# A projection's short piece in one PSUM bank, and a quarter of the values product moved ahead of the next scores

## The chip, the cores and the metric

The kernel runs on one NeuronCore of a Trainium2 chip. Its engines work side by side, each through its own queue in order: TensorE multiplies matrices (PE in the profile, with PEld for its weight loads), VectorE (DVE) and ScalarE (ACT) read results out of TensorE's accumulation memory (PSUM) and work on them, GpSimd (POOL) works on on-chip tiles only, and SyncE (SP) issues the DMA transfers. The metric is the device time of one execution in microseconds; lower is better. Before the change it is 3225.41 us, the median of three runs (3222.88 to 3227.68).

## The reference

The input is 8 images of 512 channels and 32 x 32 = 1024 positions, all in float32. Two blocks follow one another:

```python
# layer 0: multi-head attention, 8 heads of 64 channels
hn  = group_norm(x, gn1)                       # 32 groups
qkv = einsum('bchw,oc->bohw', hn, w_qkv) + b_qkv
q, k, v = split(qkv per head)
wgt = softmax(einsum('bct,bcs->bts', q*s, k*s))   # 1024 x 1024 per head, s = 64 ** -0.25
a   = einsum('bts,bcs->bct', wgt, v)
x   = x + group_norm(einsum(a, w_proj) + b_proj, gn2)
# layer 1: one attention over all 512 channels, weights normalised by row
qkv = einsum('oc,bcn->bon', w_qkv, x);  qkv = qkv / (rms over channels + 1e-4)
attn = softmax(q^T k / sqrt(512));  h = w_out @ (attn applied to v)
out = (x + h) / sqrt(2)
```

What the change touches are the projections q and k of layer 0 and the product `a`.

## The kernel before, in words

The images are taken one after the other (batch 0 to 7). For each the heads of layer 0 go in four **pairs** (j = 0 to 3, two heads side by side on the 128 rows of the array), and each pair in eight **steps** of 128 query positions, so a batch has 32 steps (i = 8 j + r). The loop over steps starts at line 1234; it collects small functions in the lists `fill`, `early` and `later`, and `Heads.step` (line 630) runs one step:

1. `softmax(i)`: for each of the two heads VectorE takes the row maxima of the scores (nm<-s) and ScalarE the exponentials (p<-s).
2. `values` of a group of two steps, on every second step from step 5 on (LAG is 5): TensorE multiplies the turned probabilities pT of the group by v, 8 blocks of positions by 2 heads, into one bank; ScalarE then writes the result to `a`.
3. the functions of `fill`: at most one piece of the next pair's projections.
4. `scores(i + 1)`: TensorE, four products of half the array's rows each.
5. `turn`: VectorE transposes the probabilities of the step before (pb<-p) and SP issues four transfers that finish the turning (pT<-pb).
6. `early`, `scale` (GpSimd divides by the row sums, p<-p), and `later`, in which GpSimd does the additions that a piece has asked for.

TensorE's order is therefore values, piece, next scores. All engines run in the order of the program, except that each waits for what it needs.

PSUM is split in two pools. Scores and other wide results take three tiles of two banks each (`ps_s`): two hold one step's scores, so the second head's scores of the next step need a tile that the first head's exponential has freed. Everything else goes through two single banks taken in turn (`ps_m`, the function `bank`, line 114).

From batch 1 on q and k of pairs 1 to 3 come from `project_seven` (line 474): by a scheme of seven products in place of eight, in four pieces n = 0 to 3. A piece is made of half-array matmuls, upper 64 rows into one bank and lower 64 rows into the other, which run two at a time. Pieces 1 to 3 have four products a half, piece 0 (the **short piece**) has two. ScalarE copies both banks of the short piece out, and GpSimd adds the copies to get one temporary, `tmp[1]`. The short piece of pair j + 1 is made at the first step of pair j: steps 0, 8 and 16. Pair 0 of the following batch uses `project_rows` in steps 24 to 31, as batch 0 does throughout.

At step 0 to 2 of a batch the last three products of layer 1 of the batch before (`Layer1.products(1, c)`, po<-e) stand in front of the piece in the same list, each in a single bank; VectorE reads each of them out in `later` (`keep`).

The weights of pair 3's and of the next batch's pair 0's projections are fetched at steps 8 and 16 (`fetch_qk`, line 257), in SP's queue in front of that step's transfers of probabilities.

Of the kernel before, what the change touches and what calls it, by code (L numbers as in the profile page):

```python
# [52 lines left out]
def attention_blocks_kernel(  # L53
# [29 lines left out]
    CI, NT, HN = C // P, N // P, N // 2  # L83
# [21 lines left out]
    PE, VE, AC, PO, SY = (InOrder(tc, e) for e in (nc.tensor, nc.vector, nc.scalar, nc.gpsimd, nc.sync))  # L105
# [8 lines left out]
    def bank(name, n=HN):  # L114
        return ps_m.tile([P, n], F32, tag="mm", name=name)

    def matmuls(pm, terms):

        for k, (lhsT, rhs) in enumerate(terms):
            PE.matmul(pm, lhsT, rhs, start=(k == 0), stop=(k == len(terms) - 1))  # L120
            if k % 2:
                yield

    def run(pieces):
        for _ in pieces:
            pass
# [32 lines left out]
    rows = const.tile([GQKV, P], F32, name="rows")  # L159
# [208 lines left out]
    RG, TG = 2, 2 * P  # L368
    NB = N // P
    STEPS, LAG = CI * NB, 5  # L370
    halves = (slice(0, D), slice(D, P))
# [62 lines left out]
    class Sums:  # L434
# [31 lines left out]

        def right(self, half, n, k):

            rows = halves[half]
            if n == 0 or (n, half) in ((1, 0), (3, 1)):  # L470
                return self.hn[rows, k, HN:] if n == 0 else self.hn[rows, k, :HN]
            return (self.t24 if n + half == 2 else self.t3)[rows, k]

    def project_seven(b, j, right):

        qk = pair.tile([P, 2, N], F32, tag="qk", name=f"qk_{b}_{j}")
        kp = qk[:, 1, :].rearrange("p (be m) -> p be m", be=4)
        w, tmp = near["qk7"][:, (j - 1) % 2], [near["v#"][:, k * HN : (k + 1) * HN] for k in range(3)]  # L480

        def turned(t):
            return t.rearrange("p (m be) -> p be m", be=4)

        q1, q2 = (qk[:, 0, th * HN : (th + 1) * HN] for th in range(2))
        k1, k2 = (kp[:, :, th * P : (th + 1) * P] for th in range(2))

        def add(to, a, b_):
            return lambda: PO.tensor_add(to, a, b_)

        adds = (
            ([add(tmp[1], tmp[1], tmp[0])], []),
            ([], []),
            ([add(q2, q2, q1), add(k2, k2, turned(q2))], [add(k1, k1, k2), add(k2, k2, turned(tmp[1]))]),
            ([add(q1, q1, tmp[0]), add(q2, q2, tmp[1])], [add(q2, q2, tmp[2])]),
        )

        def pieces():
            for n in range(4):
                pms = [bank(f"pq7_{b}_{j}_{n}_{r}") for r in range(2)]  # L500
                count, at = (CI, CI * n - 2) if n else (2, 0)
                for k in range(count):
                    for r in range(2):
                        PE.matmul(pms[r], w[halves[r], at + k, :], right(r, n, k), start=(k == 0), stop=(k == count - 1))
                if n == 0:
                    AC.copy(tmp[1], pms[0])
                    AC.copy(tmp[0], pms[1])
                elif n == 1:
                    AC.activation(q1, pms[0], AF.Identity, bias=bqs[:, j : j + 1])
                    AC.copy(k1, turned(pms[1]))  # L510
                elif n == 2:

                    AC.copy(q2, pms[0])
                    AC.activation(k2, turned(pms[1]), AF.Identity, bias=bkq[:, j : j + 1])
                else:
                    AC.copy(tmp[0], pms[1])
                    AC.copy(tmp[2], pms[0])
                yield adds[n]

        return qk, pieces()  # L520
# [30 lines left out]
    class Heads:  # L551
        def __init__(self, b, hn, v, qk):
            self.b, self.hn, self.v, self.a = b, hn, v, None
            self.qk = {0: qk}
            self.pT, self.ps, self.waiting = {}, None, None

        def scores(self, i):
            j, r = divmod(i, NB)
# [47 lines left out]
                PO.tensor_scalar(p[:, :, hh, :], p[:, :, hh, :], tot[:, hh : hh + 1], 1.0, ALU.mult, ALU.mult)  # L606
            self.waiting = (i, p)

        def values(self, g):

            j, t0 = g // (NB // RG), g % (NB // RG) * TG
            po = bank(f"po0_{self.b}_{g}", TG)
            if self.a is None:
                self.a = big(f"a_{self.b}")
            for s in range(NT):
                for hh in range(2):
                    ch = (2 * j + hh) * D
                    PE.matmul(
                        po[halves[hh], :],
                        self.v[:, s, ch : ch + D],  # L620
                        self.pT[g][:, :, :, hh, s, :],
                        start=(s == 0),
                        stop=(s == NT - 1),
                    )

            AC.activation(self.a[:, j, t0 : t0 + TG], po, AF.Identity, bias=col(BV, j))
            slots.give(f"pT_{self.b}_{g}")
            del self.pT[g]
# [110 lines left out]
    class Seven:  # L739
# [8 lines left out]
        half, drains, held = None, [], False  # L748
# [478 lines left out]
    heads, norm1, hn_next = Heads(0, x0, v0_0, qk0), None, None  # L1227
# [3 lines left out]
    for b in range(B):  # L1231
        hn, more = heads.hn, b + 1 < B
        todo, due, rest = iter(()), [], []
        for i in range(STEPS):
            j, r = divmod(i, NB)
            due = rest

            projects = (i - LAG) % RG if not b or i not in (2, 3) else i == 3

            def project():  # L1240
                nonlocal due, rest
                now, rest = next(todo, None) or ([], [])
                due = due + now

            rest, fill = [], [project] if projects else []
            early, later = [], []
            if i < CI:
                fill, later = fills[i] + fill, laters[i]
            if r == 0:
                if j + 1 < CI:  # L1250
                    heads.qk[j + 1], todo = project_seven(b, j + 1, one.next.right) if b else project_rows(
                        b, j + 1, hn, near["v#"]
                    )
                elif more:
                    qk_next, todo = project_rows(b + 1, 0, hn_next, place("spare", b))
                if j + 1 == CI:
                    slots.give(f"hn_{b}")
                    if not more:
                        o_last = big(f"o_{b}")
                        todo = project_out_half(b, heads, o_last)  # L1260
            later.append(lambda: [f() for f in due])

            if b and more and i in (1, 2, 9, 10):
                later.append(lambda: norm1.apply((1, 2, 9, 10).index(i), PO))
            if not b:


                if i == CI:
                    hn_next = big(f"hn_{b + 1}")
                    norm1 = Norm1(b + 1, hn_next)  # L1270
                if 0 <= i - CI < CI:
                    later.append(lambda: load_x(b + 1, hn_next, i - CI))
                if 0 <= i - CI - 2 < 2 * CI:
                    later.append(lambda: norm1.stats((i - CI - 2) // 2, i % 2))
                k = i - 3 * CI - 2
                if k == 0:
                    coeffs = norm1.gn.all_steps()
                    early += [norm1.aggregate, lambda: next(coeffs)]
                elif 0 < k < 8:
                    early.append(lambda: next(coeffs, None))  # L1280
                if 0 <= k - 7 < CI // 2:
                    for ci in range(2):
                        later.append(lambda ci=ci: norm1.apply(2 * (k - 7) + ci, PO))

            if b and i == NB:
                fetch_qk(CI - 1, b)
            if b and i == 2 * NB and more:
                fetch_qk(CI, b)
            if b and i == STEPS - NB - 3 and not more:
                fetch("proj", b)  # L1290
            m, odd = divmod(i - STEPS + NB, 2)
            if more and m >= 0:

                if m < 2:
                    k = slice(2 * (i - STEPS + NB), min(2 * (i - STEPS + NB) + 2, 7))
                    SY.dma_start(out=near["v7"][:, k], in_=far["v7"][:, k])
                if i == STEPS - NB:
                    tv = big(f"tv_{b + 1}").rearrange("p (k i) (h n) -> p k i h n", k=2, h=2)
                    right_v = RightSide(hn_next, tv[:, 0], tv[:, 1])
                    sums_v = (None for ci in range(CI) for _ in right_v.sum_steps(ci, PO))  # L1300
                later.append(lambda: next(sums_v, None))

            if not more and i == STEPS - 4:
                xt = big(f"x_{b}")
            if not more and m in (2, 3) and not odd:
                load_x(b, xt, m - 2)
            heads.step(i, fill, early, later)
# [123 lines left out]
```

## Time and profile before

| | |
|---|---|
| median of three runs | 3225.41 us |
| the profiled execution | 3224.11 us, of which its span is 3222.0 us |
| granted TensorE clock | 0.998 |
| PE busy | 3192.6 us, 99% of the span |
| DVE, POOL, ACT busy | 2279.2, 1253.2, 1045.5 us |
| matmul records pq (all projections by seven products) | 1176, mean 589 to 592 ns |
| ACT copies v<-pq | 84, 592 ns each |
| POOL additions v<-v, 128 x 512 | 21, 1275 ns each |

The profile is of one execution. A row of the timeline gives the start and the time in us, the engine, the line, the operation, what it writes and reads, and in brackets the idle time before it and what ended that; equal neighbours are merged (x8). Every instruction is recorded by one helper at line 34 of the program (`InOrder`), so every row says L34 and the tiles tell rows apart: s scores, nm row maxima, p probabilities, pb and pT their turned forms, pq the pieces of `project_seven`, po both kinds of values product (po<-pT in layer 0, po<-e in layer 1). One float32 matmul of the program is two records. A matmul's recorded end is modelled, so the distance between starts is the better measure.

### The profile page before, as it was taken

Reading aid. Unit: us, or ns where it says so; the run is one execution under the profiler, and the core shown is the slowest. Engines: PE = TensorE matmul, PEld = TensorE weight load, DVE = VectorE, ACT = ScalarE, POOL = GpSimd, SP = SyncE. Lnnn points to the kernel's source line nnn. Section 1 sums busy time; section 2 is a strip of 40 time slices with the busy share of each in tenths; the row PEclk is TensorE's granted clock in tenths of the full one; section 3 lists DMA queues with packets and bytes.
Section 4 is the critical chain, followed back from the end, with each engine's and each line's share of the span. In section 5 each row is a group of like instructions: output and inputs, shape, how many; then the busy total and the mean of one; then the engine's idle time right before and its main releaser. Section 6 shows DMA issues by size and latency. Waiting matters only on the chain.

```text
span 3222.0 us, 36603 instructions
## 1 busy us (share of the span) xinstructions
PE 3192.6 (99%) x13218; PEld 1645.9 (51%) x13218; DVE 2279.2 (71%) x3166; ACT 1045.5 (32%) x1813; POOL 1253.2 (39%) x1025
## 2 busy tenths in 40 slices
PE   8999999999999999999999999999999999999899
PEld 5455644455444554545544555445554556444354
DVE  5697767876678765886658866587766877578652
ACT  2453114521145211551215512254023531145210
POOL 1554224732257212671227613265223642246121
PEclk9999999999999999999999999999999999999999
DMA  6777225862168512784228832388224872158600
GB/s 203 206 204 219 76 56 155 215 200 59 56 182 226 179 43 62 203 229 142 53 85 213 224 111 52 107 215 235 92 58 112 216 220 75 30 156 211 187 7 33
DMA packets 225180, 451.57 MB, mean 140 GB/s; under 512 B 21572, under 2 KB 62056, under 8 KB 219112
## 3 DMA queue, kind: packets, MB, share of 16 engines
q1 hardware_dynamic: 224880, 449.20, 49.7%
q8 instruction: 106, 1.74, 0.2%
q14 instruction: 74, 0.61, 0.1%
q10 hardware_dynamic: 120, 0.02, 0.0%
HBM read 137.26 MB, written 29.56 MB: 52 GB/s over the span
## 4 chain that ended last, share of the span: by engine, by line
PE 93%; DMA 3%; DVE 2%; SPq 1%; issue 1%; POOL 1%; DVEq 0%; ACTq 0%; POOLq 0%
PE po L34 26%; PE s L34 13%; PE pq L34 7%; PE p_e_T L34 7%; PE p_v_T L34 6%; PE p_e_B L34 5%; PE p_v_B L34 5%; PE pqk L34 4%; PE py L34 4%; PE p_u_T L34 3%; PE p_o_T L34 3%; PE p_u_B L34 3%; PE p_o_B L34 2%; DMA pT<-pb 2%; DVE pb L34 1%; PE pv L34 1%
## 5 line engine op out<-in xcount | busy, mean ns | idle before, releaser
L34 POOL TENSOR_SCALAR p<-p,tt 128x1024 f32<-128x1024 f32 x512 | 566.0, 1118 | 742.0 <-DVE tt L34 729.6
L34 ACT ACTIVATE p<-s,nm 128x1024 f32<-128x1024 f32 x512 | 565.6, 1109 | 876.3 <-DVE nm L34 534.0
L34 DVE TENSOR_REDUCE nm<-s 128x1 f32<-128x1024 f32 x512 | 602.2, 1217 | 151.7 <-PE s L34 151.0
L34 DVE STREAM_TRANSPOSE pb<-p 128x2048 f32<-128x2048 f32 x256 | 589.9, 2304 | 50.3 <-DMA pT<-pb 27.8
L34 PE MATMUL s<-qk 64*128 64x512 f32 x2048 | 524.0, 604 | 1.1 <-POOL qk L34 0.5
L34 PE MATMUL po<-pT,v 128*64 128x256 f32 x4096 | 471.8, 383 | 3.1 <-DMA pT<-pb 3.0
L34 PE MATMUL po<-e,v 128*128 128x512 f32 x1024 | 450.8, 596 | 0.0
L34 PEld LDWEIGHTS po<-pT,v 128*64 128x64 f32 x4096 | 285.1, 137 | 221.0 <-ACT v L34 31.8
L34 PEld LDWEIGHTS s<-qk 64*128 64x128 f32 x2048 | 200.5, 186 | 250.7 <-issue 222.2
L34 PEld LDWEIGHTS po<-e,v 128*128 128x128 f32 x1024 | 191.4, 190 | 241.1 <-issue 241.1
L34 PE MATMUL pq<-hn,qk 64*128 64x512 f32 x504 | 197.1, 592 | 0.0
L34 POOL TENSOR_TENSOR esum<-esum,e 128x512 f32<-128x512 f32 x96 | 130.5, 1360 | 154.3 <-ACT e L34 151.8
L34 POOL TENSOR_TENSOR u<-u,xy 128x512 f32<-128x512 f32 x64 | 79.2, 1268 | 280.9 <-DMA xy<-far_rinv 275.4
L34 POOL TENSOR_TENSOR x<-x,o 128x1024 f32<-128x1024 f32 x21 | 52.1, 2512 | 348.5 <-ACT o L34 348.5
L34 ACT ACTIVATE e<-e,shift,rinv 128x512 f32<-128x512 f32 x128 | 100.9, 812 | 256.7 <-DVE e L34 256.7
L34 DVE TENSOR_TENSOR e<-e,p_e_T 128x512 f32<-128x512 f32 x160 | 107.0, 685 | 86.5 <-PE p_e_T L34 84.3
L34 DVE TENSOR_TENSOR v<-v,p_v_T 128x256 f32<-128x256 f32 x300 | 114.3, 417 | 68.7 <-PE p_v_T L34 50.0
L34 PE MATMUL pqk<-hn,qk 64*128 64x512 f32 (+1 forms) x672 | 158.2, 590 | 0.0
L34 PE MATMUL pq<-v,qk 64*128 64x512 f32 x336 | 150.9, 589 | 0.0
L34 PE MATMUL pq<-t,qk 64*128 64x512 f32 x336 | 150.9, 589 | 0.0
L34 PE MATMUL p_e_T<-s,t 128*128 128x512 f32 x320 | 147.8, 592 | 0.0
L34 PE MATMUL py<-x,gram 128*128 128x512 f32 x320 | 140.3, 598 | 5.4 <-issue 5.4
(222 smaller groups left out, 4096.7 us busy)
## 6 DMA issues: line engine op xcount, KB each, us to landing
pT<-pb SPq DMA_DIRECT2D x1024, 256.0 KB, 4.6
qk<-far_qk SPq DMA_DIRECT2D x21, 896.0 KB
hn<-in_x_dram SPq DMA_DIRECT2D x32, 512.0 KB, 4.6
x<-in_x_dram SPq DMA_DIRECT2D x32, 512.0 KB, 3.6
out_dram<-x SPq DMA_DIRECT2D x32, 512.0 KB, 4.6
score<-far_score SPq DMA_DIRECT2D x8, 1792.0 KB
value<-far_value SPq DMA_DIRECT2D x8, 1792.0 KB
proj<-far_proj SPq DMA_DIRECT2D x7, 1792.0 KB
```

The source lines that it names most:

```text
L34: return lambda *args, **kw: self._pin(call(*args, **kw))
```

## The change

The short piece is made with the whole array: two matmuls over all 128 rows into one bank, copied to `tmp[1]` by one ScalarE instruction; the second bank, the second copy and the addition go. `Heads.values` can now be called for part of its blocks: with `most=2` it does the first two of eight blocks and keeps the bank open for the next call. In batches 1 to 7, at the first step of pairs 1 and 2 (steps 8 and 16), such a call is put behind the short piece, that is ahead of the next scores; the rest of that group follows at the next step, where the whole of it stood.

```diff
         def right(self, half, n, k):
 
+            if n == 0:
+                return self.hn[:, k, HN:]
             rows = halves[half]
-            if n == 0 or (n, half) in ((1, 0), (3, 1)):
-                return self.hn[rows, k, HN:] if n == 0 else self.hn[rows, k, :HN]
+            if (n, half) in ((1, 0), (3, 1)):
+                return self.hn[rows, k, :HN]
...
         adds = (
-            ([add(tmp[1], tmp[1], tmp[0])], []),
+            ([], []),
...
         def pieces():
-            for n in range(4):
+            pm = bank(f"pq7_{b}_{j}_0")
+            run(matmuls(pm, [(w[:, k, :], right(None, 0, k)) for k in range(2)]))
+            AC.copy(tmp[1], pm)
+            yield adds[0]
+            for n in range(1, 4):
                 pms = [bank(f"pq7_{b}_{j}_{n}_{r}") for r in range(2)]
-                count, at = (CI, CI * n - 2) if n else (2, 0)
-                for k in range(count):
+                for k in range(CI):
                     for r in range(2):
-                        PE.matmul(pms[r], w[halves[r], at + k, :], right(r, n, k), start=(k == 0), stop=(k == count - 1))
-                if n == 0:
-                    AC.copy(tmp[1], pms[0])
-                    AC.copy(tmp[0], pms[1])
-                elif n == 1:
+                        PE.matmul(pms[r], w[halves[r], CI * n - 2 + k, :], right(r, n, k), start=(k == 0), stop=(k == CI - 1))
+                if n == 1:
...
-        def values(self, g):
+        def values(self, g, most=NT):
 
             j, t0 = g // (NB // RG), g % (NB // RG) * TG
-            po = bank(f"po0_{self.b}_{g}", TG)
+            po, s0 = self.open or (bank(f"po0_{self.b}_{g}", TG), 0)
+            s1 = min(s0 + most, NT)
+            self.open = (po, s1) if s1 < NT else None
...
-            for s in range(NT):
+            for s in range(s0, s1):
...
+            if self.open:
+                return
...
+            if b and r == 0 and 0 < j < CI - 1:
+
+                fill.append(lambda: heads.values((i + 1 - LAG) // RG, 2))
```

More of the change, by code (lines that the diff above doesn't have):

```diff
@@ L554, in __init__ @@
             self.qk = {0: qk}
-            self.pT, self.ps, self.waiting = {}, None, None
+            self.pT, self.ps, self.waiting, self.open = {}, None, None, None
         def scores(self, i):
```

## The prediction

> **What bounds the kernel now.** I read the first rows of the page, then the chain that ended last.
>
> ```profile
> span 3222.0 us, 36603 instructions
> PE 3192.6 (99%) x13218; PEld 1645.9 (51%) x13218; DVE 2279.2 (71%) x3166; ACT 1045.5 (32%) x1813; POOL 1253.2 (39%) x1025
> ...
> PE 93%; DMA 3%; DVE 2%; SPq 1%; issue 1%; POOL 1%; DVEq 0%; ACTq 0%; POOLq 0%
> ```
>
> TensorE sets the end: 93% of the chain is its own. Its 99% hides stalls, though, because a group that waits in its middle still counts as busy. So I next read its timeline around two of the steps that the change touches, both in batch 1: step 8 (the short piece of pair 2, from 546.47) and, for comparison, an ordinary step just before it.
>
> ```profile
> 528.56 1.88 PE L34 MATMUL s<-qk 64*128 64x512 f32 x8
> 530.37 3.67 PE L34 MATMUL po<-pT,v 128*64 128x256 f32 x32
> 533.97 1.99 PE L34 MATMUL s<-qk 64*128 64x512 f32 x8
> ...
> 546.47 1.88 PE L34 MATMUL pq<-hn,qk 64*128 64x512 f32 x8
> 548.18 3.04 PE L34 MATMUL s<-qk 64*128 64x512 f32 x8
> 549.24 0.30 PEld L34 LDWEIGHTS s<-qk 64*128 64x128 f32 x4 [0.87 <-ACT p L34]
> 551.15 3.67 PE L34 MATMUL po<-pT,v 128*64 128x256 f32 x32
> 554.76 1.99 PE L34 MATMUL s<-qk 64*128 64x512 f32 x8
> ```
>
> A scores group takes 1.81 us from start to start (528.56 to 530.37), and here 2.97 (548.18 to 551.15): a stall of 1.16 us. Its second head needs the third pair of banks back, which ScalarE's first exponential of step 8 frees at 549.09. After a full piece of 3.43 us TensorE comes too late to notice; after this one of 1.71 us it comes too early. The timelines of the other six batches show the same 3.04 at both steps 8 and 16: 14 stalls.
>
> Step 0, where the short piece of pair 1 stands behind a product of layer 1:
>
> ```profile
> 490.56 7.13 PE L34 MATMUL po<-e,v 128*128 128x512 f32 x16
> 497.63 2.40 PE L34 MATMUL pq<-hn,qk 64*128 64x512 f32 x7
> 498.48 0.30 PEld L34 LDWEIGHTS pq<-hn,qk 64*128 64x128 f32 x4 [0.56 <-DVE v L34]
> 499.88 2.30 PE L34 MATMUL s<-qk 64*128 64x512 f32 x7
> 502.11 7.13 PE L34 MATMUL po<-e,v 128*128 128x512 f32 x16
> ```
>
> The lower half's weight load waits 0.56 us for VectorE, which is still reading the product just finished out of the second of the two banks (0.69 us from 497.74, so until 498.43). Two half-array matmuls that should run side by side then run one after the other: from the piece to the next product 4.48 us pass, against 1.71 + 1.81 = 3.52.
>
> Then the list of waits (total us, times, longest), and from the timeline VectorE and the transfers behind step 8:
>
> ```profile
> PEld pq L34 <- DVE v L34: 3.9, 7, 0.6
> PEld s L34 <- ACT p L34: 16.2, 26, 0.9
> DVE pb L34 <- DMA pT<-pb: 27.8, 24, 2.7
> ```
>
> ```profile
> 548.95 1.04 SPq L34 DMA_DIRECT2D qk<-far_qk  x1
> ...
> 551.20 2.33 DVE L34 TENSOR_REDUCE nm<-s 128x1 f32<-128x1024 f32 x2
> 556.78 2.36 DVE L34 TENSOR_REDUCE nm<-s 128x1 f32<-128x1024 f32 x2 [0.79 <-PE s L34]
> 561.72 2.31 DVE L34 STREAM_TRANSPOSE pb<-p 128x2048 f32<-128x2048 f32 x1 [2.58 <-DMA pT<-pb]
> ```
>
> The bank wait is there in all seven batches. At step 8 a load of 896 KB of weights goes into the same queue as the probabilities, and at step 10 the transposition waits 2.58 us for them: there the transfers, not TensorE, set the time.
>
> **The change, part by part.** *Short piece, 21 times (three pairs, seven batches).* Eight half-row records become four full ones. The eight run in pairs, 1.71 us or 0.43 a pair; sixteen full ones take 7.07, 0.44 each. So TensorE's own work is the same: 0. One ScalarE copy goes (585 ns) and one GpSimd add (1275 ns in the group v<-v, x21). Both engines wait in these steps for VectorE (ACT 534.0 us before p<-s, POOL 729.6 us before its p<-p), so I cost them at 0; without that cover they would be worth 21 × 0.585 = 12.3 and 26.8 us. No DMA is added, dropped or moved, and SP's order stays.
>
> *Step 0, seven times.* One bank instead of two: the piece takes the bank whose product was read long before, and VectorE's read of the other hides behind it; the next product takes that other bank at about 501.1, long after it is free. The cost goes from 4.48 to 3.52 us: −0.96, × 7 = **−6.7** (a change of array shape, priced below, only moves from before the piece to behind it). Steps 1 and 2 hold 7.07 us of products each beside 6.2 us of VectorE work (reductions 2.36, transposition 2.30, 0.12, reading out 1.39), so TensorE stays the pacer and the gain is handed on; what follows, SP's load at step 8 too, is issued relative to it.
>
> *Steps 8 and 16, fourteen times.* A quarter of a values group (32 records, 3.60 us: 0.90) moves ahead of the stalled scores. With 546.47 + 1.71 + 0.90 the scores start at 549.08 or later, beside the exponential's end at 549.09: the stall is filled. From the piece's start to the scores of step 10 it is now 8.29 us; without the 1.17 of stall it is 7.12.
>
> Against it stands a rule. The rows: scores between two half-row groups take 1.71 us, between two full-array groups 1.92 (488.64 to 490.56), so one change between array shapes costs 0.10. The Trainium skill says that changing the tiling mode drains TensorE ("TensorEngine Tiling (Array Packing)", Tiling Modes, Key Properties). Here the order scores, piece, scores, values, scores has two changes of shape; the new one (half rows, full, half columns, half rows, half columns, half rows) has five. Three more at 0.10 are 0.3. The rule has no price; if each exposed the fixed latency of a single warm matmul, 398 cycles at 2.4 GHz or 0.166 us ("TensorE: Matmul & The Clock Gate", Single matmul latency), they would be 0.5, an estimate. I take the row: 1.17 − 0.3 = 0.87 each (with the rule 0.67, and the final sum 1.1 us less).
>
> The edit adds one wait: the quarter reads probabilities whose four transfers were issued from 540.60 to about 543.2, landing 4.6 us later, by 547.8; TensorE is there at 548.3. Half a microsecond of room. In the stretch 535 to 600 us the landings are 4.6, 5.1 and 7.7 us (least, middle, most), so the cost lies between 0 and 2.6 us; most lie near 5, so I take 0 except where the trace is worse. Behind it in TensorE's order stand the next scores, and VectorE's reductions wait for those.
>
> What is late next? *Step 8:* the reductions of step 9 (551.20) stood behind VectorE's own work, not behind scores, and don't move; those of step 10 can come 0.79 earlier, and then the transposition still starts at 561.72. The scores of step 12 stand behind it: in batches 1 to 6 they last 2.01 to 3.10 us against 1.99 unstalled, so they are already held and TensorE's early arrival is spent in waiting: 0. In batch 7 that group is not stretched and the DMA wait is 0.97: about 0.4 of the 0.87 stays. *Step 16:* the load is 512 KB; in batches 1, 2, 6 and 7 no DMA wait follows in the two steps behind: 0.87 × 4 = 3.5. In batch 3 the transposition of step 18 already waits 1.11 us, in batch 4 that of step 17 0.57, in batch 5 the quarter's own transfers land about 1 us late: I keep 0.4, 0.6 and 0.2. Together 4.7.
>
> Sum: −6.7 − 4.7 − 0.4 = **−11.8 us**. The profiled execution took 3224.11 us (span 3222.0 and 2.1 around it), 1.3 less than the median of 3225.41; subtracted from the median: **3213.6**.
>
> **The rivals.**
> *The transfers don't take step 8's gain.* If the probabilities land earlier because the steps before are shorter, batches 1 to 6 keep 0.87 each: 5.2 more, 3208.4. Against it: the load is issued at the same place and the transposition behind it ended on a DMA.
> *Only step 0 pays.* The quarters wait 0.5 to 1 us for their transfers, or the DMA waits behind step 16 grow (batches 3 to 5 show them): 3225.4 − 6.7 = 3218.7. For it: only half a microsecond of room.
> *The transfers take everything back.* The heads' stage keeps the DMA engines 75% busy (488 to 690 us); if the 0.96 of step 0 also ends in longer waits for pT at step 10, only about 2 us remain: 3223, no change.
> *Slower.* One mechanism: the early quarter stands in TensorE's order ahead of scores it doesn't need, and waits for the landing. Above 0.87 us of lateness a place loses; with 14 places the total turns to a loss beyond 0.87 + 6.7/14 = 1.35 us at each. At the 7.7 us landing (2.6 late) it is 14 × 1.73 − 6.7 = +17.5, 3243. Against it: the transfers in question are issued before the weight load, and landed in 4.6 to 5.1.
>
> **How the numbers follow.** Main case 0.60 (3210 to 3217.5 by itself), step 8 paying too 0.10, only step 0 0.17, all taken back 0.08, slower 0.05. About 0.2%, 6.5 us, is what a measurement of this kernel can tell from no change. Below 3219 lie the first two and half of the third: faster 0.79; same 0.16; slower 0.05. The range 3207 to 3221 takes in the first two cases and most of the third.
>
> **What would show it.** Step 0: no wait of pq for DVE v in the list, and about 3.5 us between the two products. Step 16: the piece as four full records, eight of po, a scores group of 1.9 instead of 3.04, 24 of po. Step 8: the same, but the wait of pb for pT at step 10 longer by 0.8 and the scores of step 12 stretched to about 3 or more. POOL without v<-v. The forecast is wrong if po waits for pT at steps 8 and 16, if the stall reappears at step 18 or 20, or if the waits for pT grow by the whole gain.

## The result, and the profile after

The changed kernel takes 3214.94 us, the median of five runs (3211.29 to 3218.32); the kernel before takes 3226.09 in the runs beside it. The ratio is 0.9968 with a 95% interval of 0.9956 to 0.9979, so about 10.3 us faster (0.32%). The forecast was 11.8 us, 3213.6. The profiled execution took 3213.27 us with a span of 3211.5, 10.5 less than the span before.

First the page's opening rows and its chain, after the change:

```profile
span 3211.5 us, 36365 instructions
PE 3181.4 (99%) x13134; PEld 1635.6 (51%) x13134; DVE 2280.4 (71%) x3166; ACT 1034.1 (32%) x1792; POOL 1229.2 (38%) x1004
...
PE 95%; DMA 2%; DVE 2%; SPq 1%; issue 1%; POOL 0%; ACT 0%; DVEq 0%; ACTq 0%; POOLq 0%
```

21 ScalarE instructions and 21 of GpSimd are gone (1813 to 1792, 1025 to 1004) and 84 matmul records (13218 to 13134), as the diff says. TensorE is still the chain, with 95% of it.

Step 8 of batch 1, TensorE's timeline after (start, us):

```profile
544.54 1.99 PE L34 MATMUL s<-qk 64*128 64x512 f32 x8
546.45 1.98 PE L34 MATMUL pq<-hn,qk 128*128 128x512 f32 x4
548.37 1.08 PE L34 MATMUL po<-pT,v 128*64 128x256 f32 x8
549.38 1.99 PE L34 MATMUL s<-qk 64*128 64x512 f32 x8
...
551.30 2.81 PE L34 MATMUL po<-pT,v 128*64 128x256 f32 x24
554.04 1.99 PE L34 MATMUL s<-qk 64*128 64x512 f32 x8
```

The scores group that stretched over 3.04 us lasts 1.99: the stall is gone. Eight records of values stand in front of it and 24 behind it, and nothing waits for pT. What is worth reading closely is the distance from start to start, because all 14 places (seven batches, steps 8 and 16) show the same to 0.01 us:

| from start to start, us | before | after |
|---|---|---|
| scores before the piece | 1.82 | 1.92 |
| short piece | 1.72 | 1.91 |
| eight values records | | 1.01 |
| scores after the piece | 2.97 (1.81 and a stall) | 1.92 |
| the rest of the values | 3.60 | 2.74 |
| sum | 10.11 | 9.50 |

A place gains 0.61, not 0.87. Over the seven batches that is 4.2 us at step 8 (0.605 each, before rounding) and as much at step 16.

Step 0 of the same batch, between two products of layer 1:

```profile
491.30 7.13 PE L34 MATMUL po<-e,v 128*128 128x512 f32 x16
498.27 1.88 PE L34 MATMUL pq<-hn,qk 128*128 128x512 f32 x4
500.08 1.99 PE L34 MATMUL s<-qk 64*128 64x512 f32 x8
502.00 2.41 PE L34 MATMUL po<-e,v 128*128 128x512 f32 x5
```

From the one product to the next it is now 10.70 us (491.30 to 502.00); before it was 11.55 (490.56 to 502.11). The piece follows at once, the wait of pq for DVE v is in no row of the list of waits, and 0.85 us is gained in each of the seven batches.

Behind step 8, the load, VectorE, and TensorE at step 11 and 12:

```profile
549.01 0.96 SPq L34 DMA_DIRECT2D qk<-far_qk  x1
...
556.14 2.33 DVE L34 TENSOR_REDUCE nm<-s 128x1 f32<-128x1024 f32 x2
561.36 2.31 DVE L34 STREAM_TRANSPOSE pb<-p 128x2048 f32<-128x2048 f32 x1 [2.88 <-DMA pT<-pb]
...
563.63 2.33 DVE L34 TENSOR_REDUCE nm<-s 128x1 f32<-128x1024 f32 x2
...
561.37 3.67 PE L34 MATMUL po<-pT,v 128*64 128x256 f32 x32 [0.19 <-DMA pT<-pb]
564.97 2.77 PE L34 MATMUL s<-qk 64*128 64x512 f32 x7
...
566.19 0.30 PEld L34 LDWEIGHTS s<-qk 64*128 64x128 f32 x4 [0.92 <-ACT p L34]
...
567.58 0.59 PE L34 MATMUL s<-qk 64*128 64x512 f32 x1
```

This is how the transfers reach TensorE: the transposition of step 10 waits for them, the reductions of step 11 (563.63) stand behind it in VectorE's order, the exponential needs their maxima, and the second head of the scores of step 12 waits 0.92 us for that exponential (566.19).

Counted from the batch's first scores (489.38 here, 488.64 before), the reductions of step 10 come 1.38 us earlier than before, step 0's 0.85 among it, but the transposition behind them only 1.10, after 2.88 us of waiting for the transfers in place of 2.58; and the scores of step 12 last from 564.97 to 568.17, 3.2 us. Over the seven batches that transposition's wait grew from 12.2 to 15.9 us. Set side by side, the starts of the scores groups of the two profiles lose 0.10 to 0.97 us between steps 11 and 16 in six batches and gain 0.21 in one (batch 3), 2.8 us together. So of the 4.2 us of step 8 about 1.4 are left in this profile. Its account is 5.9 (step 0) + 8.5 (steps 8 and 16) − 2.8 = 11.6, of which 10.5 are left at the end; 0.7 is lost by the end of batch 0, which the change doesn't touch, and 0.8 behind the last heads, with a few tenths back in between. These last differences are of two single executions, and their cause is open.

### The profile page after: what moved, and what is told of

The parts are those of the page before. It is cut to its first block, busy times and chain, and to the rows that moved or that the text cites. A ratio compares the mean times of both kernels' runs of the same rounds, so it can differ in the third digit from the quotient of the medians.

```text
span 3211.5 us, 36365 instructions
## 1 busy us (share of the span) xinstructions
PE 3181.4 (99%) x13134; PEld 1635.6 (51%) x13134; DVE 2280.4 (71%) x3166; ACT 1034.1 (32%) x1792; POOL 1229.2 (38%) x1004
## 3 DMA queue, kind: packets, MB, share of 16 engines
q8 instruction: 105, 1.72, 0.2%
## 4 chain that ended last, share of the span: by engine, by line
PE 95%; DMA 2%; DVE 2%; SPq 1%; issue 1%; POOL 0%; ACT 0%; DVEq 0%; ACTq 0%; POOLq 0%
PE po L34 27%; PE s L34 14%; PE pq L34 7%; PE p_e_T L34 7%; PE p_v_T L34 6%; PE p_e_B L34 5%; PE p_v_B L34 5%; PE pqk L34 5%; PE py L34 4%; PE p_u_T L34 3%; PE p_o_T L34 3%; PE p_u_B L34 3%; PE p_o_B L34 2%; DMA pT<-pb 1%; PE pv L34 1%; PE pG L34 1%
## 5 line engine op out<-in xcount | busy, mean ns | idle before, releaser
L34 PE MATMUL s<-qk 64*128 64x512 f32 x2048 | 509.1, 605 | 0.4 <-ACT p L34 0.2
L34 PEld LDWEIGHTS s<-qk 64*128 64x128 f32 x2048 | 192.6, 186 | 241.8 <-issue 216.6
L34 PE MATMUL pq<-hn,qk 64*128 64x512 f32 (+1 forms) x420 | 191.8, 593 | 0.0
```

Source lines behind the costliest of these rows:

```text
L34: return lambda *args, **kw: self._pin(call(*args, **kw))
```

## The experiments

Each is timed against the kernel before; a ratio below 1 is faster than before, and 0.001 is 3.2 us. The changed kernel's own is 0.9968.

**The short piece alone.** The lines in the step loop that call for the quarter are taken out of the changed kernel.

```diff
-            if b and r == 0 and 0 < j < CI - 1:
-
-                fill.append(lambda: heads.values((i + 1 - LAG) // RG, 2))
```

> The changed kernel without the moved quarter: only the short piece in one bank. My theory: step 0 keeps its 0.85 us in each of seven batches, 6.0 us; at steps 8 and 16 the scores stall again until the exponential ends (scores groups of about 3 us), so nothing there. About 3220 against 3226 of the kernel before. Rival (the dropped ScalarE copy and GpSimd addition are the gain): some gain at steps 8 and 16 too, near the changed kernel's 3215. Rival (step 0's wait only moves): no change from 3226.

Measured: 3218.01 us, ratio 0.9981 (0.9972 to 0.9990), 6.1 us less than before. TensorE at step 8:

```profile
543.63 1.99 PE L34 MATMUL s<-qk 64*128 64x512 f32 x8
545.55 1.98 PE L34 MATMUL pq<-hn,qk 128*128 128x512 f32 x4
547.46 2.74 PE L34 MATMUL s<-qk 64*128 64x512 f32 x8
```

The scores still stall (2.74), a little less than before because the piece itself has become 0.2 and the scores ahead of it 0.1 longer; the scores of step 10 start at the same distance as before. So the bank is worth 6 us, all of it at step 0.

**The moved quarter alone.** The changed kernel with the two-bank piece put back (its operands and its addition too, which are not shown).

```diff
...
-            pm = bank(f"pq7_{b}_{j}_0")
-            run(matmuls(pm, [(w[:, k, :], right(None, 0, k)) for k in range(2)]))
-            AC.copy(tmp[1], pm)
-            yield adds[0]
-            for n in range(1, 4):
+            for n in range(4):
                 pms = [bank(f"pq7_{b}_{j}_{n}_{r}") for r in range(2)]
...
+                if n == 0:
+                    AC.copy(tmp[1], pms[0])
+                    AC.copy(tmp[0], pms[1])
```

> The kernel before with the moved quarter alone: the short piece still in two banks of half rows, and added by GpSimd. My theory: the quarter then needs the bank that ScalarE reads out only after both exponentials of the step (about 550.8 in the before profile's time, TensorE is there at 548.2), and the next scores wait behind it; the scores of step 10 start some 1.5 us later than before at step 16, at step 8 part of that hides in front of the DMA wait. 12 to 24 us slower than before, 3238 to 3250. Rival (the bank doesn't matter, the moved quarter alone fills the stall): about 4 us faster than before, 3222.

Measured: 3254.29 us, ratio 1.0092 (1.0079 to 1.0106), 29.7 us slower. Step 8 there:

```profile
546.68 1.88 PE L34 MATMUL pq<-hn,qk 64*128 64x512 f32 x8
...
550.39 1.07 ACT L34 COPY v<-pq 128x512 f32<-128x512 f32 x2
551.02 1.08 PE L34 MATMUL po<-pT,v 128*64 128x256 f32 x8 [2.46 <-ACT v L34]
```

The quarter waits 2.46 us for the first of the two copies, which stands in ScalarE's order behind both exponentials. Each of the 14 places loses 1.73 us up to the scores of step 10 or 18, and little of it hid at step 8: I expected too much cover there, since the transfers had held the scores behind it by no more than 0 to 1.1 us a batch, 3.5 in all. The profiled execution, the fastest of the four, is 24.5 us longer in span than that of the kernel before; the others go up to 3260.37 us while the granted clock falls from 0.997 to 0.994, so a part of the 29.7 goes with the clock and not with the wait. The two halves of the change aren't two gains to be added: the move is a loss without the single bank.

**The quarter at step 16 only.**

```diff
-            if b and r == 0 and 0 < j < CI - 1:
+            if b and r == 0 and j == CI - 2:
```

> The changed kernel with the quarter moved at step 16 only, not at step 8. My theory (the transfers behind the 896 KB load take step 8's gain at steps 12 to 14): 0.4 to 1.4 us more than the changed kernel, not to be told from it. Rival (step 8 pays in full, 0.6 us in each of seven batches): 4.2 us more than the changed kernel, about 3219.

Measured: 3213.61 us, ratio 0.9965 (0.9951 to 0.9978), the same as the changed kernel. By the medians nothing of step 8's 4.2 us reaches the end, but the two intervals together leave about 5 us open either way, so this run alone doesn't exclude the rival; the profiles, set side by side at the end of this section, say that about a third of it does. Step 16 gives 0.9981 − 0.9965, about 5 us.

**The load of step 8 cut into seven.** In the changed kernel the 896 KB go in parts of 128 KB at steps 8 to 14, which is early enough for their first use at step 16.

```diff
-            if b and i == NB:
-                fetch_qk(CI - 1, b)
+            if b and NB <= i < 2 * NB - 1:
+                k = slice(2 * (i - NB), 2 * (i - NB) + 2)
+                SY.dma_start(out=near["qk7"][:, 0, k], in_=far["qk7"][:, k, (CI - 2) * P : (CI - 1) * P])
```

> The changed kernel with the 896 KB load of step 8 cut into seven of 128 KB, one in each of steps 8 to 14. My theory: the transposition of step 10 no longer waits 1 to 3 us for the transfers, the scores of steps 12 and 13 are not held (2.0 us or less instead of up to 3.28), and step 8's gain stays: 3 to 8 us less than the changed kernel, 3207 to 3212. Rival (TensorE or VectorE holds those scores whatever the transfers do, or the smaller loads cost the same in sum): the same as the changed kernel, 3215.

Measured: 3207.26 us, ratio 0.9945 (0.9933 to 0.9958), 7.4 us less than the changed kernel by the two ratios, with some 5 us of uncertainty. Batch 1 once more:

```profile
548.74 1.61 SPq L34 DMA_DIRECT2D qk<-far_qk  x1
...
555.05 0.65 SPq L34 DMA_DIRECT2D qk<-far_qk  x1
...
559.37 1.04 SPq L34 DMA_DIRECT2D qk<-far_qk  x1
...
558.50 2.31 DVE L34 STREAM_TRANSPOSE pb<-p 128x2048 f32<-128x2048 f32 x1 [0.29 <-DMA pT<-pb]
...
564.51 1.99 PE L34 MATMUL s<-qk 64*128 64x512 f32 x8
```

The same transposition waits 0.29 us instead of 2.88, and the scores of step 12 last 1.99. The same bytes on the same queue, spread over seven steps, no longer stand in front of the probabilities. Over the seven batches that wait falls from 15.9 to 4.4 us; in batch 5 it is still 2.31, and there the scores of step 12 are still held.

**The same cut in the kernel before.**

> The kernel before with the load of step 8 alone cut into seven. My theory (in the kernel before the transfers already held the scores of steps 12 and 13 a little, and step 8's stall of 1.16 us was paid in part out of the same wait): the scores of step 12 unheld, 1 to 4 us less than before. Rival (the cut load is a gain of its own and doesn't need the change): the whole 7 to 8 us that it brought to the changed kernel.

Measured: 3221.67 us, ratio 0.9989 (0.9980 to 0.9997), 3.5 us less. So of the 7.4 us that the cut brings to the changed kernel about half was there to be had without the change; the other half, some 3.9, would be what the transfers took of step 8's gain. The interval of this run allows 1.0 to 6.5, so the division is rough. The profile is sharper: the waits at step 10 are gone in all seven batches, and the scores of steps 11 to 16, held for 3.5 us before, are not held at all.

**Half a group instead of a quarter.** `heads.values(..., 4)` in place of 2.

> The changed kernel with half of the group moved (16 records of 32) instead of a quarter. The same number of changes of array shape, so TensorE's own sum stays; but the scores of step 9 begin 0.9 us later, VectorE's reductions of step 9 with them, and the scores of step 10 are held by the exponential of step 9. My theory: about 0.6 us lost again at step 16 in each batch, at step 8 partly in front of the DMA wait: 3 to 8 us more than the changed kernel. Rival (what is moved only has to be enough): no difference.

Measured: 3219.34 us, ratio 0.9982 (0.9976 to 0.9989), 4.5 us more than the changed kernel. In TensorE's timeline of step 9 the hold is back at the next scores:

```profile
552.20 2.35 PE L34 MATMUL s<-qk 64*128 64x512 f32 x7
553.00 0.35 PEld L34 LDWEIGHTS s<-qk 64*128 64x128 f32 x4 [0.51 <-ACT p L34]
```

TensorE's sum up to the scores of step 10 is the same (0.61 gained), but those scores are held by ScalarE, and 0.79 us is lost again by the scores of steps 12 and 20 in all seven batches. At step 8 most of this hides in front of the wait for the transfers, as expected.

**The dropped work given back.** In the changed kernel ScalarE copies the bank a second time, into `tmp[0]`, and GpSimd adds `tmp[1]` to it; nothing reads the sum.

> The changed kernel with the work that it dropped given back to ScalarE and GpSimd, 21 times each: a second copy of the bank (0.585 us) and an addition of 128 x 512 (1.275 us), whose result is overwritten later and used by nothing. My theory: both are hidden, no difference from the changed kernel within 2 us. Rival (the short piece's gain is the dropped work): up to 12 us from the copies or 27 us from the additions.

Measured: 3211.71 us, ratio 0.9964 (0.9951 to 0.9976), as the changed kernel. Both are hidden.

**Both loads cut.** As the cut of step 8, and the 512 KB of step 16 in four parts of 128 KB at steps 16 to 19.

> The changed kernel with the load of step 8 cut into seven and the 512 KB load of step 16 cut into four (steps 16 to 19). My theory: after step 16 no scores were held in the changed kernel, so the second cut brings nothing, within 1.5 us of the kernel with the first cut alone, about 3207. Rival (the transposition's DMA waits at step 18 of up to 1.67 us cost time): 2 to 4 us less than that, 3204.

Measured: 3206.63 us, ratio 0.9943 (0.9930 to 0.9955): the same as with the first cut alone, though the intervals are too wide to exclude the 2 to 4 us of the rival. The profiles do: with the first cut alone no scores between steps 18 and 24 come late, so the load of step 16 held none of them up. These two are the fastest kernels of the study, about 18 us below the kernel before.

**All profiles side by side.** The scores of step 16 start 32.01 us after those of step 10 wherever nothing is late, and so do those of step 24 after those of step 18. What a profile shows beyond that is time in which the scores were held; here it is summed over batches 1 to 7, from one execution of each kernel.

| us held | steps 10 to 16 | steps 18 to 24 |
|---|---|---|
| before | 3.5 | 0.0 |
| short piece alone | 1.3 | 0.3 |
| quarter at step 16 only | 4.6 | 0.0 |
| changed | 6.3 | 0.2 |
| changed, dropped work given back | 5.8 | 0.3 |
| changed, half a group | 7.9 | 5.6 |
| changed, load of step 8 cut | 1.1 | 0.0 |
| before, load of step 8 cut | 0.0 | 0.0 |
| both loads cut | 0.0 | 0.9 (once, in batch 5) |
| moved quarter alone | 0.0 | 0.0 |

With the load whole, the three kernels without a quarter at step 8 are held for 1.3 to 4.6 us behind it (3.1 on average), the two with a quarter for about 6. So the transfers take about 3 of the 4.2 us that step 8 gains, and some 1.3 stay. With the load cut hardly any of the held time is left, with or without the move. The moved quarter alone is never held behind the load because its scores are already late.

## Why the prediction was right, and where its terms were off

*Step 0, −6.7.* Right. The bank wait is gone and the piece alone gives 6.1 us. The profile shows 0.85 a batch instead of 0.96. I had the scores between the piece and the product at 1.81; between two full-array groups they take 1.92, as the row that I cited myself says. The moved change of shape was free, as I had counted it: the product ahead of the piece takes 6.97 in place of 7.07, the piece 1.81 in place of 1.71.

*The dropped copies and additions, 0.* Right: given back, they cost nothing. The waits of 534 and 730 us that I cited for it are sums over the whole kernel and not of these steps; it is this run that shows it.

*Step 8, −0.4.* Right in its mechanism and too low in its size. The transfers take most of this gain and give it back when the load is cut, but about 1.3 us stay, by the table above. The predicted signs are there: the wait at step 10 is longer (by 0.3 to 1.1 us in six batches, shorter in batch 3) and the scores of step 12 last 2.25 to 3.28 us in six of seven. Batch by batch I was right for batch 7 (0.34 kept, 0.4 forecast) and wrong for batches 1, 3 and 5, of which I expected nothing: by step 16 they are 0.25, 0.81 and 0.50 ahead; batch 4 lost 0.38 more than it gained. But this sets two single profiles side by side, and which batch is held differs from profile to profile.

*Step 16, −4.7.* The sum is near what was found (4.0 in the profile, about 5 by the two ratios), but by two errors against each other, so that it came so near is luck. The stall of 1.17 was filled. The three added changes of array shape were put at 0.10 each from one row; they cost 0.55 together (1.92 + 1.91 + 1.01 + 1.92 + 2.74 = 9.50 against 1.82 + 1.72 + 1.81 + 3.60 = 8.95 without the stall), 0.18 each. That is the mis-sized term. The estimate from the latency of a single warm matmul in the Trainium skill ("TensorE: Matmul & The Clock Gate", Single matmul latency), 0.5, set beside the row and not taken, was the nearer one. The page gives that latency for bf16 and this kernel is float32, and the rows here don't show the same cost at each change, so the nearness doesn't show that this latency is what a change costs. On the other side I had taken 1.4 us off for batches 3 to 5, where transfers were late in the profile before; in the profile after no quarter waits at any of the 14 places, and only batch 3 lost any of step 16's gain, 0.2 us, by the scores of steps 19 to 21 (I had taken off 0.47 there). VectorE still waits for the transfers (up to 1.67 us at step 18, in batch 3), but in the other batches TensorE's scores stand far enough behind.

*The added wait.* Half a microsecond of room was enough. The longer scores and piece ahead of the quarter also bring TensorE there later, by 0.3 us.

*The rival that step 8 pays too* holds for about a third of step 8's gain, by the profiles; *only step 0 pays* falls with the difference between the step-16-only run and the piece alone; *the transfers take everything back* falls with the piece alone, which keeps step 0's 6 us. The slower rival's mechanism, a quarter in front of scores that it holds up, does exist: it is what the move without the single bank shows, with ScalarE's copy in the place of the transfers.

## What to carry to other kernels

A gain in front of a wait for something else isn't a gain: before an idle slot is filled, look some steps further for the wait that ends on a transfer, and where a large load stands in the same queue, cut it up first; here that gave 7.4 us by the ratios, and the moved quarter 4.2, each with some 4 to 5 us of uncertainty. When two banks are used in turn, the bank that a new piece of work will take decides whether the move is a gain or a loss of 1.7 us a place. Small fillings of TensorE must pay for the changes of array shape that they bring: here 0.55 of a stall of 1.16.

## What the runs showed of the hardware

A change of array shape costs more than one row suggested, and the cost depends on the neighbours. Scores (half rows) take 1.72 between half-row groups, 1.82 with one foreign neighbour and 1.92 with two; four full-array records take 1.72 in a run of their own kind (0.43 from start to start), 1.81 before half rows at step 0, and 1.91 both before half columns and, with the piece alone, between two half-row groups. A values group of 32 records takes 3.60, but cut in 8 and 24 it takes 1.01 + 2.74 = 3.75. That these differences are the price of the changes of shape is read from the rows; no run here changes the shape and nothing else.

Cutting one load of 896 KB into seven on the same queue moved the same bytes and took 2.6 us off the wait of the transfers behind it in the batch shown, though in that batch each part cost SP 0.65 to 1.6 us to issue (up to 2.0 in others). SP's own order had room for it: at steps 8 to 10 of that batch the issue of the part had ended before the transposition whose result the next transfers carry.
